# A three-layer interaction network on one core: reordering the preparation of its weights

## The chip, the core and the metric

The kernel runs on one core of a Trainium2 chip. The core has TensorE (PE, matrix products, which write to the accumulation memory PSUM), VectorE (DVE), ScalarE (ACT) and GpSimd (POOL) for element-wise work, SyncE (SP) as a further issuer of transfers, and 16 DMA engines that move data between DRAM and the on-chip memory SBUF. PSUM has eight banks of 128 rows by 512 float32 columns. The engines run on their own and wait for each other by semaphores. The metric is the device time of one execution in microseconds (us), the median of several runs; less is better.

## The reference

For each of 1024 samples there is a matrix X0 of 39 fields by 64 embedding columns. Three layers each form all products of a field of the layer's input with a field of X0 and mix them with weights. The sums over the embedding columns of all three layers go through one linear layer.

```python
B, F, E = (1024, 39, 64); HID = [64, 64, 64]        # B is 1024 in the inputs
def _cin_layer(Xk, X0, W, b):
    Wr = W.reshape(O, Hk, Fdim)
    return jnp.einsum('bhe,bfe,ohf->boe', Xk, X0, Wr) + b[None, :, None]
Xk = X0
for W, b in ((W0, b0), (W1, b1), (W2, b2)):
    Xk = _cin_layer(Xk, X0, W, b)
    outs.append(Xk.sum(axis=-1))
y = concatenate(outs, axis=-1) @ fc_w.T + fc_b
```

All data are float32. Only the sum over the last layer is wanted, so a kernel may multiply weights together beforehand: fc_w's last third into W2 gives a matrix v2 (64 by 39), v2 into W1 gives a table T (fields by fields by 64), and only W0 and T then meet the data.

## The kernel before

It has a prologue, which builds a table of weights `wa`, and a stream of main products, which multiplies `wa` by products of fields. The samples are taken in 32 blocks of 32 samples (2048 columns). For a block, GpSimd gathers rows of x into four rolled copies `r` (and, for two blocks at a time, `u` and `v`), VectorE multiplies two of them into a tile `p`, and TensorE multiplies `p` by one chunk of `wa` in four quarters of 512 columns, into four PSUM banks `po`. Six chunks belong to each block and a seventh, of half height, to two blocks.

The prologue, by engine in program order (cuts are marked):

```python
psum = tile_pool(name="psum", bufs=8, space=PSUM)      # eight banks, taken in turn
...
nc.vector.memset(ones, 1.0)
nc.vector.memset(zeros, 0.0)                            # 128 x 512
...
load(0)                                                 # x of block 0, on SyncE
nc.scalar.dma_start(fcrow, fc_w)
nc.scalar.dma_start(w2s, w2...)
load_ones(0, nc.scalar)
nc.scalar.dma_start(w0s[0:F], w0v[:, 0 : NW * H])       # NW = 20 fields
nc.sync.dma_start(w0s[H : H + F, ...], w0v[:, NW * H : F * H])
for s, engine in enumerate((nc.sync, nc.scalar)):
    engine.dma_start(w1s[H * s : H * s + H], w1[...])
...
def spin(n, to):                                        # a dummy product of zeros
    nc.tensor.matmul(to[:, 0:n], zeros[:, 0:128], zeros[:, 0:n], start=True, stop=True)
spin(512, pr)
...                                                     # index lists; GpSimd starts the gathers
nc.tensor.matmul(small[:, 0:1], fcrow2, one)            # fc turned into a column
nc.vector.tensor_scalar(fc2[:, 0::32], mask, small[:, 0:1], None, ALU.mult)
spin(128, pr)
for k in ...: turn_row(small[...], k)                   # five more turned rows
for k in range(2):                                      # v2 from W2: 2 banks x 4 column groups
    for u in range(4):
        nc.tensor.matmul(pv[k][32 * u : 32 * u + 32, 0:320], fc2[...], w2v[...])
for k in range(NW // 2):                                # W0 turned, alternating row groups
    for s in range(2):
        nc.tensor.transpose(pw[s][...], w0s[H * s : H * s + F, ...], unit[...])
...                                                     # v2 copied; more index lists
def untwine(half, a, n, src, width):
    for s, copy in enumerate((nc.vector.tensor_copy, nc.scalar.copy)):
        copy(bothv[H * half :..., a + s : a + n : 2, 0:width], src[H * s : H * s + H, ...])
for s, (a, n) in enumerate(((0, NW), (NW, F - NW))):
    untwine(0, a, n, pw[s], F)                          # W0 into `both`
for s in range(2):                                      # T = v2 x W1, fields 0 to 31
    for k in range(2):
        nc.tensor.matmul(pt[s][H * k : H * k + H], v2[rows], w1v[rows, NA * k : ...])
for s in range(2):                                      # fields 32 to 38, one bank for both s
    nc.tensor.matmul(pr[rows, 0 : 32 * NR], v2[rows], w1v[rows, 2 * NA : F, :])
spin(128, small)
for s, copy in enumerate(copies): copy(part[:, :, ...], pt[s]...)
for s, copy in enumerate(copies): copy(rest[:, :, ...], pr[H * s : ...]...)
for k in range(3):                                      # T turned: part, part, rest
    for a in range(0, n, 2): nc.tensor.transpose(to[...], src[rows, a : a + m, :], unit[...])
    untwine(1, NA * k, n, to, FT)                       # T into `both`
for _ in range(2): spin(256, small)
```

Then come the first three chunks. `weight_rows` adds entries of `both` into `pairs`, `weight_turn` turns that by TensorE and ScalarE copies it into `wa`:

```python
for k, (n, c) in enumerate(steps[:3]):
    weight_rows(c)
    if not k:
        weight_turn(c)
        spin(256, small)
    product(n, c, halves[0], p[n, c])                   # 1024 columns of p
for n, c in steps[:3]:
    product(n, c, halves[1], p[n, c])
n, c = steps[3]; weight_rows(c); p[n, c] = product(n, c)
for k, (n, c) in enumerate(steps[:3]):                  # TensorE: quarter 0, turn, quarter 1
    multiply(n, c, p[n, c], (0,))
    if k < 2: weight_turn(steps[k + 1][1])
    multiply(n, c, p[n, c], (1,))
...                                                     # quarters 2, 3; then all other chunks
```

Of the kernel before, what the change touches and what calls it, by code (L numbers as in the profile page):

```python
# [98 lines left out]
def cin_kernel(ctx: ExitStack, tc: tile.TileContext, x, w0t, b0, w1, b1, w2, b2, fc_w, fc_b, out):  # L99
# [72 lines left out]
    with prep as prep:  # L172
# [8 lines left out]
        ones = prep.tile([16, 2, 128], F32, name="ones")  # L181
        zeros = prep.tile([128, MM], F32, name="zeros")
        warm = prep.tile([1, 1], F32, name="warm")
# [7 lines left out]


        nc.vector.memset(ones, 1.0)
        nc.vector.memset(zeros, 0.0)  # L194
        nc.vector.memset(fc2, 0.0)
# [3 lines left out]
        def load_ones(k, engine):  # L199
            engine.dma_start(xd[k][F::FT].rearrange("r (p c) -> p r c", c=128), ones)  # L200

        load(0)
        nc.scalar.dma_start(fcrow, fc_w)
        nc.scalar.dma_start(w2s, w2.rearrange("o (s n) -> (o s) n", s=2))
        load_ones(0, nc.scalar)
        w0v = w0t.rearrange("b a h -> b (a h)")
        nc.scalar.dma_start(w0s[0:F], w0v[:, 0 : NW * H])
        nc.sync.dma_start(w0s[H : H + F, 0 : (F - NW) * H], w0v[:, NW * H : F * H])  # L208
        for s, engine in enumerate((nc.sync, nc.scalar)):
# [13 lines left out]

        pv = [bank("pv") for _ in range(2)]
        small = bank("small")
        pw = [bank("pw") for _ in range(2)]
        pt = [bank("pt") for _ in range(2)]
        pr = bank("pr")


        def spin(n, to):
            nc.tensor.matmul(to[:, 0:n], zeros[:, 0:128], zeros[:, 0:n], start=True, stop=True)  # L232

        spin(512, pr)


# [60 lines left out]
        nc.vector.tensor_scalar(unit, apart, 0, None, ALU.is_equal)  # L297
        spin(128, pr)
        for k in range(3):
            turn_row(small[0:H, k + 1 : k + 2], k)  # L300
        for k in range(2):
            turn_row(small[H:128, k + 4 : k + 5], k)

# [10 lines left out]
        for k in range(2):  # L314
            for u in range(4):
                f0 = u // 2 * 19 + k * 10
                nc.tensor.matmul(  # L317
                    pv[k][32 * u : 32 * u + 32, 0:320],
                    fc2[:, u % 2 * 32 : u % 2 * 32 + 32],
                    w2v[:, f0 : f0 + 10, :],  # L320
                    start=True,
                    stop=True,
                )

        for k in range(NW // 2):
            for s in range(2):
                n = min(128, (F - NW * s) * H - k * 128)
# [11 lines left out]
        for s in range(2):  # L339
            rows = slice(H * s, H * s + H)  # L340
            nc.vector.tensor_copy(v2[rows, 0:20], column[0:H])
            nc.scalar.copy(v2[rows, 20:F], column[H:128, 1:20])
        nc.scalar.copy(fc, small[0:H, 1:4])
        nc.scalar.copy(fc0s[H:128], small[H:128, 4:5])

# [18 lines left out]

        def untwine(half, a, n, src, width):

            for s, copy in enumerate(copies):
                m = (n + 1 - s) // 2
                copy(  # L369
                    bothv[H * half : H * half + H, a + s : a + n : 2, 0:width],  # L370
                    src[H * s : H * s + H, 0 : m * FT].rearrange("p (a b) -> p a b", b=FT)[
                        :, :, 0:width
                    ],
                )

        for s, (a, n) in enumerate(((0, NW), (NW, F - NW))):
            untwine(0, a, n, pw[s], F)
        w1v = w1s.rearrange("o (h f) -> o f h", f=F)
        for s in range(2):
            rows = slice(H * s, H * s + H)  # L380
            for k in range(2):
                nc.tensor.matmul(  # L382
                    pt[s][H * k : H * k + H],
                    v2[rows],
                    w1v[rows, NA * k : NA * (k + 1), :],
                    start=True,
                    stop=True,
                )
        for s in range(2):
            rows = slice(H * s, H * s + H)  # L390
            nc.tensor.matmul(  # L391
                pr[rows, 0 : 32 * NR], v2[rows], w1v[rows, 2 * NA : F, :], start=True, stop=True
            )
        spin(128, small)
        for s, copy in enumerate(copies):
            at = slice(32 * s, 32 * s + 32)
            copy(part[:, :, at], pt[s].rearrange("b (a h) -> b a h", h=32))
        for s, copy in enumerate(copies):
            at = slice(32 * s, 32 * s + 32)
            copy(  # L400
                rest[:, :, at],
                pr[H * s : H * s + H, 0 : 32 * NR].rearrange("b (a h) -> b a h", h=32),
            )
        for k in range(3):
            src = part if k < 2 else rest
            rows = slice(H * (k % 2), H * (k % 2) + FT)
            n = NA if k < 2 else NR
            to = (pv[0], pv[1], pr)[k]
            for a in range(0, n, 2):
# [5 lines left out]
                )  # L415
            untwine(1, NA * k, n, to, FT)
        for _ in range(2):
            spin(256, small)
        first = [prods.tile([128, BLK], F32, name="p", tag="p") for _ in range(3)]
# [131 lines left out]
    for k, (n, c) in enumerate(steps[:3]):  # L551
        p[n, c] = first[k]
        weight_rows(c)
        if not k:
            weight_turn(c)
            spin(256, small)
        product(n, c, halves[0], p[n, c])
    for n, c in steps[:3]:
# [100 lines left out]
```

## Time and profile before

| | |
|---|---|
| median of 3 runs | 751.73 us (751.16 to 751.74) |
| span of the profiled execution | 748.3 us |
| PE busy | 739.5 us (99%) |
| DVE busy | 643.5 us (86%) |
| ACT busy | 163.8 us (22%) |
| POOL busy | 319.3 us (43%) |
| mean DMA rate | 241 GB/s |
| mean granted TensorE clock | 0.995 |

Busy time is the time in which an engine has an instruction in work. Matmuls overlap and their ends are modelled, so a busy TensorE is not one at its peak. The page cuts the span in 40 slices, each of 18.7 us here, and gives the busy share of each in tenths. A row of the timeline gives start, length, engine, line of the kernel, operation, output and inputs, count, and in brackets the idle time before it with what ended it. Lines 369, 397, 400 and 411 are the copies into `both`, `part` and `rest` and the transposes of T; 382 and 391 are the products of v2 and W1; 328 the transposes of W0; 431 the sums in `pairs`; 466 and 467 the turned chunk and its copy; 482 the main products; 232 the dummies; 166 the products of fields.

### The profile page before, as it was taken

How to read it: one execution, taken by the hardware profiler on the slowest of the kernel's cores; microseconds unless marked ns; L12 is line 12 of the kernel's file. 1: busy time of each engine (PE TensorE's matmuls, PEld its weight loads, DVE VectorE, ACT ScalarE, POOL GpSimd, SP SyncE). 2: the span in 40 equal slices, each digit the busy share in tenths (PEclk: the TensorE clock that was granted, in tenths of full speed). 3: DMA queues.
4: the chain of work that ended last, by engine and by line, in shares of the span. 5: the costliest groups of instructions: out<-in, count | busy, mean ns of one | idle time of the engine just before them, and what ended most of it. 6: DMA issues, size and time to landing. Idle time of an engine off the chain costs nothing.

```text
span 748.3 us, 5266 instructions
## 1 busy us (share of the span) xinstructions
PE 739.5 (99%) x1903; PEld 322.7 (43%) x1903; DVE 643.5 (86%) x509; ACT 163.8 (22%) x223; POOL 319.3 (43%) x193
## 2 busy tenths in 40 slices
PE   7999999999999999999999999999999999999998
PEld 3444444444444444444444444444444444444443
DVE  5998899888889888898888889888899888898885
ACT  2132211221212222212221212222112221212222
POOL 5778633336353253633436243263532436243100
PEclk8999999999999999999999999999999999999999
DMA  8789975875757776575875757776565855737400
GB/s 268 270 304 412 330 290 171 330 259 205 289 164 280 252 293 250 178 294 176 338 255 201 288 166 281 259 278 252 185 275 202 336 224 179 295 138 288 168 1 0
DMA packets 58791, 180.07 MB, mean 241 GB/s; under 512 B 37079, under 2 KB 37176, under 8 KB 38669
## 3 DMA queue, kind: packets, MB, share of 16 engines
q0 software_dynamic: 24160, 169.39, 59.6%
q1 hardware_dynamic: 34277, 9.17, 5.3%
q10 hardware_dynamic: 328, 1.18, 0.6%
q8 instruction: 15, 0.25, 0.1%
q14 instruction: 11, 0.09, 0.0%
HBM read 179.66 MB, written 10.28 MB: 254 GB/s over the span
## 4 chain that ended last, share of the span: by engine, by line
PE 97%; DMA 1%; DVE 0%; issue 0%; SPq 0%; ACT 0%
PE po L482 96%; DMA w1s<-in_w 1%; PE pv L411 0%; PE pt L382 0%; PE small L232 0%; PE tr L466 0%; SPq L118 0%; ACT both L369 0%; PE pr L391 0%; SPq L208 0%; DVE g L521 0%; DVE sums L523 0%; ACT zq L520 0%; DVE pairs L431 0%; DVE both L369 0%
## 5 line engine op out<-in xcount | busy, mean ns | idle before, releaser
L482 PE MATMUL po<-p,wa 128*128 128x512 f32 (+1 forms) x1792 | 721.9, 595 | 0.0
L166 DVE TENSOR_TENSOR p<-r 128x2048 f32<-128x2048 f32 (+1 forms) x195 | 434.8, 2257 | 85.4 <-PE po L482 84.6
L482 PEld LDWEIGHTS po<-p,wa 128*128 128x128 f32 (+1 forms) x1792 | 313.5, 190 | 405.0 <-issue 383.5
L125 POOL DMA_INDIRECT r<-xd,lists x131 | 256.3, 1956 | 361.1 <-DVE p L166 330.7
L501 ACT ACTIVATE z<-po,fc0s 64x512 f32<-64x512 f32 x124 | 84.7, 683 | 356.4 <-PE po L482 349.5
L495 ACT COPY g<-u 39x1024 f32<-39x1024 f32 x64 | 66.6, 1043 | 180.7 <-DVE sums L512 180.6
L507 DVE SCALAR_TENSOR_TENSOR g<-po,b0s,z 64x512 f32<-64x512 f32 x124 | 86.4, 734 | 0.0
L512 DVE TENSOR_REDUCE sums<-g 103x16 f32<-103x1024 f32 x62 | 75.6, 1220 | 2.2
L125 POOL DMA_INDIRECT u<-xd,lists x16 | 33.0, 2062 | 9.8 <-DMA xd<-in_x 5.2
L168 DVE TENSOR_TENSOR p<-u,v 128x2048 f32<-128x2048 f32 x16 | 36.6, 2285 | 0.0
L125 POOL DMA_INDIRECT v<-xd,lists x16 | 20.3, 1269 | 4.9 <-issue 4.9
L521 DVE SCALAR_TENSOR_TENSOR g<-po,b0s,zq 64x512 f32<-64x512 f32 x4 | 3.0, 743 | 5.3 <-ACT zq L520 5.3
L467 ACT COPY wa<-tr 128x128 f32<-128x128 f32 x7 | 1.9, 266 | 18.9 <-PE tr L466 18.9
L431 DVE TENSOR_TENSOR pairs<-both 128x6 f32<-128x6 f32 (+27 forms) x50 | 5.4, 177 | 0.4 <-ACT both L369 0.4
L118 POOL DMA_DIRECT2D xd<-in_x x5 | 5.2, 1047 | 0.0
L520 ACT ACTIVATE zq<-po,fc0s 64x512 f32<-64x512 f32 x4 | 2.7, 683 | 10.2 <-PE po L482 10.2
L232 PE MATMUL pr<-zeros 128*128 128x512 f32 (+1 forms) x4 | 2.9, 822 | 1.7 <-DVE zeros L194 1.7
L232 PE MATMUL small<-zeros 128*128 128x256 f32 (+1 forms) x8 | 3.7, 591 | 0.0
L382 PE MATMUL pt<-w1s,v 64*64 64x512 f32 x8 | 2.2, 1107 | 1.4 <-DMA w1s<-in_w 1.4
L334 DVE STREAM_TRANSPOSE blocks<-pv 128x320 f32<-128x320 f32 x2 | 1.0, 516 | 2.2 <-PE pv L317 2.2
L523 DVE TENSOR_REDUCE sums<-g 103x8 f32<-103x512 f32 x4 | 2.7, 686 | 0.1
L610 PE MATMUL py<-sums,wfin 103*1 103x512 f32 (+2 forms) x6 | 2.1, 448 | 0.6 <-DVE sums L523 0.6
(95 smaller groups left out, 43.8 us busy)
## 6 DMA issues: line engine op xcount, KB each, us to landing
xd<-in_x SPq DMA_DIRECT2D x27, 312.0 KB
r<-xd,lists POOLq DMA_INDIRECT x131
xd<-in_x POOLq DMA_DIRECT2D x5, 312.0 KB
w2s<-in_w ACTq DMA_DIRECT2D x1, 624.0 KB
w1s<-in_w ACTq DMA_DIRECT2D x1, 312.0 KB
w1s<-in_w SPq DMA_DIRECT2D x1, 312.0 KB
u<-xd,lists POOLq DMA_INDIRECT x16
v<-xd,lists POOLq DMA_INDIRECT x16
```

Of the source, the lines that this page charges most:

```text
L118: engine.dma_start(xd[n // 2 % NTAB][first : first + F].rearrange("f (b e) -> f b e", e=E), xv[:, n * BB : (n + 1) * BB, :],)
L125: nc.gpsimd.indirect_dma_start(dst[:, cols], None, table, bass.IndirectOffsetOnAxis(ap=lists[:, k : k + 1], axis=0), element_offset=cols.s ...
L166: nc.vector.tensor_tensor(p[:, cols], r[:, i, cols], r[:, k, cols], ALU.mult)
L168: nc.vector.tensor_tensor(p, ut[n // 2 % 2], vt[n // 2 % 2], ALU.mult)
L232: nc.tensor.matmul(to[:, 0:n], zeros[:, 0:128], zeros[:, 0:n], start=True, stop=True)
L431: nc.vector.tensor_tensor(out, diagonal(a, b, sa, sb), diagonal(b, a, sb, sa), ALU.add)
L482: nc.tensor.matmul(po[n + h][m], wa[w, c, :], p[w, bass.ts(m, MM)], start=c == opens[n + h], stop=c == closes[n + h],)
L495: nc.scalar.copy(gt[H : H + F], ut[n // 2 % 2][h : h + F, bass.ts(m, SUB)])
L501: nc.scalar.activation(z[m // 2][:, bass.ts(m % 2, MM)], po[n][m][H:128], AF.Identity, bias=fc0s[H:128])
L507: nc.vector.scalar_tensor_tensor(gt[0:H, at], po[n][m][0:H], b0s, z[m // 2][:, at], ALU.add, ALU.mult)
L512: nc.vector.tensor_reduce(sums[:, b_at : b_at + SB], gt.rearrange("p (b e) -> p b e", e=E), AX.X, ALU.add)
L521: nc.vector.scalar_tensor_tensor(gt[0:H], po[n][m][0:H], b0s, t, ALU.add, ALU.mult)
```

## The change

It reorders the prologue and leaves the main stream and the arithmetic as they are. Its aims are these.

- W2 goes first on ScalarE's queue and the small fc row to SyncE's, so that W2 and, behind it, W1 arrive sooner. Both parts of W0 go on ScalarE's queue.
- W0's transposes run one row group after the other and no longer alternate.
- The last seven fields of T are multiplied, copied and turned first. Each row group of these products gets its own bank.
- Each copying engine gets a bank of its own: VectorE unpacks one and ScalarE the other, where before both shared each bank. The fields of the first 32 come in another order so that each engine's copies cover a connected range of fields.
- All dummies have 256 columns, write to a bank `idle` that nothing else uses, and come in pairs. `zeros` is half as wide and is set first.
- The turned rows of fc come after W2's products, and the copies of them to SBUF after the first three half products.
- The first product of fields is cut in two of 512 columns, so that TensorE's first quarter has its data sooner.

The diff, cut to its core:

```diff
-        zeros = prep.tile([128, MM], F32, name="zeros")
+        zeros = prep.tile([128, MM // 2], F32, name="zeros")
+        nc.vector.memset(zeros, 0.0)
         nc.vector.memset(ones, 1.0)
-        nc.vector.memset(zeros, 0.0)
...
+        nc.sync.dma_start(fcrow, fc_w)
+        nc.scalar.dma_start(w2s, w2.rearrange("o (s n) -> (o s) n", s=2))
         load(0)
-        nc.scalar.dma_start(fcrow, fc_w)
-        nc.scalar.dma_start(w2s, w2.rearrange("o (s n) -> (o s) n", s=2))
         load_ones(0, nc.scalar)
-        nc.scalar.dma_start(w0s[0:F], w0v[:, 0 : NW * H])
-        nc.sync.dma_start(w0s[H : H + F, 0 : (F - NW) * H], w0v[:, NW * H : F * H])
+        for s, n in enumerate((NW, F - NW)):
+            nc.scalar.dma_start(w0s[H * s : H * s + F, 0 : n * H], ...)
...
+        pt = [bank("pt") for _ in range(2)]
+        idle = bank("idle")
+        pw = [bank("pw") for _ in range(2)]
         small = bank("small")
-        pw = [bank("pw") for _ in range(2)]
-        pt = [bank("pt") for _ in range(2)]
-        pr = bank("pr")
...
+        def spin(n=1):
+            for _ in range(n):
+                nc.tensor.matmul(idle[:, 0 : MM // 2], zeros[:, 0:128], zeros, start=True, stop=True)
+        spin(2)
...
-        spin(128, pr)
-        for k in range(3): turn_row(...)            # these five go behind W2's products
+        spin(2)
...
-        for k in range(NW // 2):
-            for s in range(2):
+        for s in range(2):
+            for k in range(NW // 2):
                 nc.tensor.transpose(pw[s]...)
...
         for s, (a, n) in enumerate(((0, NW), (NW, F - NW))):
-            untwine(0, a, n, pw[s], F)
+            untwine(copies[s], 0, a, n, 1, pw[s], F)
+        for s in range(2):
+            nc.tensor.matmul(pv[s][rows, 0 : 32 * NR], v2[rows], w1v[rows, 2 * NA : F, :])
         for s in range(2):
             for k in range(2):
                 nc.tensor.matmul(pt[s][H * k : H * k + H], v2[rows],
-                    w1v[rows, NA * k : NA * (k + 1), :])
+                    w1v[rows, NA * k : NA * (k + 1), :].rearrange("o (t j) h -> o j t h", t=2))
-        for s in range(2):
-            nc.tensor.matmul(pr[rows, 0 : 32 * NR], v2[rows], w1v[rows, 2 * NA : F, :])
-        spin(128, small)
-        # copies: part from pt, then rest from pr; turned and unpacked: part, part, rest
+        # copies: rest from pv, then part from pt
+        turn_fields(pt[0], rest, slice(0, FT), NR)
+        untwine(copies[0], 1, 2 * NA, NR, 1, pt[0], FT)
+        for k in range(2):
+            turn_fields(pw[k], part, slice(H * k, H * k + FT), NA)
+        for k in range(2):
+            untwine(copies[k], 1, NA * k, NA, NA // 2, pw[k], FT)
+        spin(2)
...
             weight_turn(c)
-            spin(256, small)
-        product(n, c, halves[0], p[n, c])
+            spin()
+            for m in range(2):
+                product(n, c, slice(m * MM, (m + 1) * MM), p[n, c])
+        else:
+            product(n, c, halves[0], p[n, c])
+    nc.scalar.copy(fc, small[0:H, 1:4])
+    nc.scalar.copy(fc0s[H:128], small[H:128, 4:5])
```

## The prediction

> **What bounds the kernel now.** I read the page first, for who is busy, then the chain of waits, then the timeline of the first 40 us.
>
> ```profile
> PE   7999999999999999999999999999999999999998
> PEclk8999999999999999999999999999999999999999
> L482 PE MATMUL po<-p,wa 128*128 128x512 f32 (+1 forms) x1792 | 721.9, 595 | 0.0
> ```
>
> The main products (line 482) fill 721.9 of 748.3 us with no idle time in front. They are 896 products in two records each. A full one advances the timeline by 0.86 us (two records of 0.43), so nothing that the change does not touch can shrink: its arithmetic stays. What is left is the first slice of PE, the 7, and the clock, the 8. The chain of waits, cut to that stretch (start, length, what):
>
> ```profile
> 2.62 7.63 DMA w1s<-in_w
> 10.25 0.75 issue
> 11.00 2.18 PE pt L382 x8
> 13.18 0.82 PE pr L391 x4
> ...
> 15.31 2.27 PE pv L411 x16
> ...
> 19.27 0.58 DVE pairs L431 x5
> ...
> 21.29 1.19 PE po L482 x2
> ```
>
> So the prologue is one chain: W1 lands, is multiplied by v2, turned, unpacked into `both`, added into `pairs`, and the first main product leaves at 21.12 us. The ends of matmuls are modelled, so I take true ends from who could start on them. From the timeline:
>
> ```profile
> 8.83 0.79 PE L328 MATMUL pw<-unit,w0s 39*128 39x39 f32 x20 [0.55 <-DMA w0s<-in_w0t]
> 11.77 1.03 DVE L369 COPY both<-pw 64x390 f32<-64x390 f32 x2 [1.09 <-remote]
> 13.92 0.69 DVE L397 COPY part<-pt 128x512 f32<-128x512 f32 x1 [1.13 <-PE pt L382]
> 14.67 0.58 ACT L397 COPY part<-pt 128x512 f32<-128x512 f32 x1 [1.39 <-PE pr L391]
> 16.79 0.38 DVE L400 COPY rest<-pr 64x224 f32<-64x224 f32 x1 [2.18 <-PE pv L411]
> 17.21 0.34 ACT L400 COPY rest<-pr 64x224 f32<-64x224 f32 x1 [1.96 <-issue]
> 17.60 0.88 DVE L369 COPY both<-pv 64x320 f32<-64x320 f32 x2 [0.43 <-PE pv L411]
> 19.13 0.71 DVE L431 TENSOR_TENSOR pairs<-both 128x36 f32<-128x36 f32 x6 [0.41 <-ACT both L369]
> 19.76 1.22 DVE L166 TENSOR_TENSOR p<-r 128x1024 f32<-128x1024 f32 x1
> ```
>
> Three things are to be seen. VectorE, idle for 1.09 us, reads W0's transposes only at 11.77, so 20 of them, alternating between two row groups, took 11.77 - 8.83 = 2.9 us, 0.145 us each, and W1's products, ready at 11.00, really ran from about 11.7. VectorE then waits for `rest` until 16.79, over 2 us after `pt` was readable (14.67): the small product into the shared bank `pr` was late. And ScalarE's copies start just behind VectorE's (17.21 after 17.17).
>
> **What the Trainium skill says.** "TensorE: Matmul & The Clock Gate", Part 1: the clock is halved by default, judged in free-running windows of about 3.4 us, and sustained activity releases it. The trace agrees: the granted clock is 0.50 from 11.4 to 14.8 and from 18.2 to 21.65 us, full between and after. "TensorEngine Tiling (Array Packing)", Gotcha 1: different row tiles cannot access one PSUM bank at the same time. The late `pr`, written by both row groups, is in keeping with it; the trace doesn't prove it. "PSUM — Partial Sum Buffer", PSUM bank collisions: engines must be kept apart by bank and quadrant; the tight order of the two copies of `pr` agrees. "DMA: Bandwidth & Descriptors", Queues, rings and completion order: each DMA engine serves its queues in turn, packet by packet. In the trace x's first 256-byte packets move at 4.28 us, just before W2's last end (4.74), although x was issued first.
>
> **The change, part by part.**
>
> W2 and W1 sooner. W2's issue moves to the head of ScalarE's queue, 1.27 to 0.74 us, fcrow goes to SyncE. From 2 to 10 us the DMA engines are 0.84 to 1.08 busy in the table by stage, and the bytes are the same, so the whole train moves by about 0.5: W1 is usable at 10.5 instead of 11.0, and x with its gathers also about 0.5 sooner.
>
> W0 group by group. The four transposes of `rest` (17.61, 0.41 us, one row group) suggest 0.23 us latency and 0.06 each after that. At that pace 20 cost 1.4 us, and with W0's second half landing near 9.0 they end near 10.2, ahead of W1. W1's products then start at 10.5 instead of 11.7: 1.2 us sooner.
>
> Last fields first, bank per row group. `rest` is 224 columns in two passes. At the slow clock a 512-column pass takes 0.85 us (the first dummy: two passes and about 0.37 latency are its 2.08), so these take 2 x 0.37 = 0.75. `pt` needs 14.67 - 11.7 = 2.95 until ScalarE may read, as before. So ScalarE's copy of `part` starts at 10.5 + 0.75 + 2.95 = 14.2 (before 14.67) and ends at 14.8 (0.58). What is won at the start is mostly spent on `rest` in front, but the 2 us of `pr` behind it vanish: `rest` is copied near 11.7, beside `pt`.
>
> Transposes and unpacking. Sixteen transposes: 14.8 + 0.23 + 16 x 0.063 = 16.05. Then each engine has its own bank and its own range of fields; ScalarE's two copies (0.42 each) end at 16.9. `pairs` starts near 16.95 instead of 19.13: 2.2 us sooner.
>
> Half of the first product. `pairs` 0.71, then 512 columns instead of 1024 (half of 1.22, 0.61): the first main product goes at 16.95 + 0.71 + 0.61 + 0.1 = 18.4 instead of 21.12, 2.7 us sooner. Not all of that is kept. VectorE must deliver three sets of `pairs` and three half products before the third chunk's product; before, this took from 19.13 to 24.80, 5.7 us, so now it is ready at 16.95 + 5.7 = 22.65. TensorE took it at 25.1 before. That is 2.4 us sooner, and from there I count TensorE as unbroken again.
>
> Dummies. Columns of dummies go from 1280 to 1792. In front of W2 they cost nothing as long as W2 lands no sooner (about 4.6); the two pairs later sit in waiting time. The copies of fc and fc0s (0.15 each) and the turned rows (0.82 for five) leave the path to W2, onto time in which TensorE waits for W1.
>
> Sum if all of it works: 2.4 us. Discounts: 40% that transposes cost 0.14 each whatever their order (two groups of 16 and 10 on the path: about 1.2 us back, 0.5 expected), and a clock that may be slow behind 18.2, below, with little of it expected net, since before also began in slow clock. I predict 1.9 us off: 751.73 - 1.9 = 749.8.
>
> **The rivals.**
>
> Transposes are bound by their weight loads. They read 0.139 us each in the load rows, and 16 of them from 15.31 to 17.60 is 0.14 too. Against it stand the four of `rest`. If it holds, W0 ends near 11.3, `part`'s last transpose near 17.2, `pairs` starts at 18.1, and the time is about 750.8.
>
> The clock falls. With dummies ending early (after the last transposes, not beside the copies), the window from 14.8 to 18.2 may be half empty, as before's was (it lost the clock at 18.2). Then the first four quarters run at 1.7 instead of 0.86 us up to 21.65, TensorE and no longer VectorE is late at the third chunk by about 1.2 us, and the time is about 750.6. For the change: its dummies are longer. If instead the clock is full from 14.8 on, and W1's products too run full, the time is near 748.5.
>
> The gathers of block 1 become the bound. In the timeline its second product starts at 42.82 after 0.63 us on the DMA of r. This landing moves only 0.5 while the rest moves 2. But counting 0.86 per product TensorE takes that chunk near 49.9, and it is ready at 45.1; 4.8 of reserve, so 2 to 3 are left. If I am wrong there, gathers eat the whole gain: 751.5.
>
> W1 is not sooner, as packets of x or of the gathers go first: the gain shrinks by 0.5, to 750.3.
>
> **Range and chances.** All rivals that I see give 748.5 to 751.5; three runs of before span 0.6. I give 748.2 to 751.3 for 8 in 10. A change of 2% is 15 us, and the whole prologue in front of the first main product is 21 us, so faster by that much is out of reach (0.005); slower needs a stream that breaks later on (0.01). Within 2%: 0.985.
>
> **What would show it.** Right: W1's products near 10.5; VectorE's copy of `pw` ready before 10.5; `rest` copied before `part`; `pairs` near 17; first main product near 18.4, with one gap of a few tenths before the third chunk; main products unchanged at 722 us or a little above. Each step is wrong if its time stays where it was: transposes of `part` still 2.2 us long, W1's products still at 11, or a clock of 0.50 behind 18.2. The prediction fails as a whole if TensorE waits for r or for products beyond 25 us, or if the prologue's saving passes 3.5 us.

## The result and the profile after

The kernel after takes 751.41 us (median of four runs, 749.11 to 752.54), beside 751.74 of the kernel before on the same chip: ratio 0.9993 with a 95% interval of 0.9969 to 1.0018. A later measurement with 13 runs of after and 51 of before gives 750.65 against 751.23, 0.9990 (0.9982 to 0.9998). So the change takes off 0.1%, about 0.6 us, where 1.9 were predicted. Only the second interval excludes no change, and barely.

From the page of the kernel after, the same two rows that the prediction began with:

```profile
PE   7999999999999999999999999999999999999998
PEclk8899999999999999999999999999999999999999
```

TensorE is as full as before. The second slice of the clock, 18.75 to 37.5 us, has fallen from 9 to 8. The rest of the answer lies again in front of the first main product. The chain of waits up to there (start, length, what):

```profile
2.15 9.83 DMA w1s<-in_w
...
12.12 0.74 PE pv L383 x2
...
15.17 0.76 issue
15.93 0.38 PE pt L409 x4
16.31 0.78 PE pw L409 x16
17.09 1.65 PE idle L233 x4
...
18.76 0.43 ACT both L371
...
19.80 0.59 DVE pairs L434 x5
...
21.82 1.71 PE po L485 x2
```

W1 is longer on its way (9.83 us, before 7.63) and its products start at 12.12 instead of 11.00. The 16 transposes of `part` are short, 0.78 us. Then comes a piece that has no business here: 1.65 us "PE idle L233", dummy products, and ScalarE leaves only behind them. The timeline (start, length, engine, line, operation, and in brackets the idle time before it and who ended it):

```profile
8.67 1.30 PE L329 MATMUL pw<-unit,w0s 39*128 39x39 f32 x20
10.01 0.94 ACT L371 COPY both<-pw 64x390 f32<-64x390 f32 x2 [0.42 <-PE pw L329]
11.77 1.17 POOL L125 DMA_INDIRECT r<-xd,lists  x1 [8.67 <-DVE both L371]
13.18 0.38 DVE L398 COPY rest<-pv 64x224 f32<-64x224 f32 x1 [1.53 <-PE pv L383]
15.09 0.69 DVE L404 COPY part<-pt 128x512 f32<-128x512 f32 x1 [1.52 <-PE pt L389]
15.20 0.59 ACT L404 COPY part<-pt 128x512 f32<-128x512 f32 x1 [1.55 <-PE pt L389]
16.98 0.99 DVE L371 COPY both<-pw 64x320 f32<-64x320 f32 x2
18.76 0.86 ACT L371 COPY both<-pw 64x320 f32<-64x320 f32 x2 [2.97 <-PE idle L233]
19.66 0.72 DVE L434 TENSOR_TENSOR pairs<-both 128x36 f32<-128x36 f32 x6 [1.68 <-ACT both L371]
21.62 1.91 PE L485 MATMUL po<-p,wa 128*128 128x512 f32 x2
```

Half of the plan works. W0's transposes are read at 10.01 (before 11.77), `rest` at 13.18 (16.79) and `part`'s products by ScalarE at 15.20 (14.67), although W1 came 1.1 us later. The second bank of `part`'s transposes undoes it: VectorE reads the first at 16.98, ScalarE's copy of the second, turned 0.3 us behind it, starts at 18.76. `pairs` starts at 19.66 (19.13) and the first main product at 21.62 (21.12). The first row gather is issued at 11.77; the prediction had it half a microsecond sooner than in before, where its row is:

```profile
7.44 1.17 POOL L125 DMA_INDIRECT r<-xd,lists  x1 [4.34 <-DMA xd<-in_x]
```

From the table by stage (stretch, its length, busy time and count of PE, PEld, DVE, ACT and POOL, granted TensorE clock, DMA share, GB/s), two stretches of after and then one of before:

```profile
18.00:21.40 3.40, 1.03 (x4) 0.69 (x4) 1.74 (x8) 1.44 (x6) 2.87 (x3) 0.50 0.87 287
21.40:24.85 3.45, 3.45 (x6) 1.66 (x6) 3.45 (x19) 0.66 (x4) 1.18 (x1) 0.50 1.07 377
21.60:25.00 3.40, 3.40 (x10) 1.34 (x9) 3.40 (x14) 0.53 (x2) 2.30 (x2) 0.99 0.53 183
```

The clock is 0.50 from 18.0 to 24.85 us in after; in before it is 0.50 from 18.2 to 21.64 and full behind it. So the main products of after ran at half clock for their first 3.2 us, those of before for 0.5.

**One sum that holds for every trace.** The third chunk's first product is the point from which the prediction took TensorE as unbroken. I read its start from each trace and take it from that execution's own time:

| profiled execution | first main product | third chunk | its time | time minus third chunk |
|---|---|---|---|---|
| before | 21.12 | 25.11 | 750.06 | 724.95 |
| after | 21.62 | 26.88 | 751.83 | 724.95 |
| again (after, once more) | 21.71 | 26.82 | 751.77 | 724.95 |
| dma_before | 23.48 | 27.91 | 752.86 | 724.95 |
| no_late_dummy | 21.51 | 27.41 | 752.38 | 724.97 |
| before_w0_grouped | 21.65 | 26.53 | 751.49 | 724.96 |
| after_gathers_held | 26.26 | 32.34 | 757.28 | 724.94 |
| dense_end | 20.97 | 25.32 | 750.34 | 725.02 |
| before_four_gathers | 19.53 | 23.34 | 749.53 | 726.19 |
| four_gathers_hold_by_act | 19.19 | 23.01 | 748.04 | 725.03 |

The four traces left out of the table give 724.95, 724.97, 724.96 and 726.34. From the third chunk on everything is 725.0 us, to a tenth, but for two traces with 1.2 and 1.4 more, which are explained below. A prologue's microsecond is worth a full microsecond, and "hidden later on" is no answer here. The table also shows that the page of before belongs to one of its shorter executions, 750.06 against a median of 751.73, and that of after to one 0.4 above its median: two traces must be compared with their own times, not with the medians.

### The profile page after: what moved, and what is told of

It is laid out like the page before. It is cut to its first block, busy times and chain, and to the rows that moved or that the text cites. A ratio compares the mean times of both kernels' runs of the same rounds, so it can differ in the third digit from the quotient of the medians.

```text
span 750.1 us, 5270 instructions
## 1 busy us (share of the span) xinstructions
PE 740.6 (99%) x1905; PEld 324.1 (43%) x1905; DVE 643.9 (86%) x511; ACT 163.8 (22%) x222; POOL 324.4 (43%) x193
## 4 chain that ended last, share of the span: by engine, by line
PE 97%; DMA 1%; DVE 0%; issue 0%; ACT 0%; SPq 0%; ACTq 0%
PE po L485 96%; DMA w1s<-in_w 1%; PE idle L233 0%; PE pt L389 0%; PE tr L469 0%; SPq L118 0%; PE pv L383 0%; ACT both L371 0%; PE pw L409 0%; DVE g L524 0%; DVE sums L526 0%; ACT zq L523 0%; DVE pairs L434 0%; PE pt L409 0%; SPq L203 0%
## 5 line engine op out<-in xcount | busy, mean ns | idle before, releaser
L166 DVE TENSOR_TENSOR p<-r 128x2048 f32<-128x2048 f32 (+2 forms) x196 | 434.9, 2247 | 86.3 <-PE po L485 83.6
L125 POOL DMA_INDIRECT r<-xd,lists x131 | 265.2, 2025 | 357.1 <-DVE p L166 325.2
L125 POOL DMA_INDIRECT u<-xd,lists x16 | 32.3, 2022 | 10.5 <-DMA xd<-in_x 5.9
L125 POOL DMA_INDIRECT v<-xd,lists x16 | 17.2, 1074 | 4.9 <-issue 4.9
L233 PE MATMUL idle<-zeros 128*128 128x256 f32 x14 | 6.3, 591 | 1.2 <-DVE zeros L193 1.2
L523 ACT ACTIVATE zq<-po,fc0s 64x512 f32<-64x512 f32 x4 | 2.7, 684 | 10.2 <-PE po L485 10.2
L469 PE MATMUL tr<-unit,pairs 128*128 128x128 f32 x7 | 2.2, 319 | 2.4 <-DVE pairs L434 2.4
L233 PEld LDWEIGHTS idle<-zeros 128*128 128x128 f32 x14 | 3.6, 289 | 1.7 <-DVE zeros L193 1.2
```

Source lines behind the costliest of these rows:

```text
L125: nc.gpsimd.indirect_dma_start(dst[:, cols], None, table, bass.IndirectOffsetOnAxis(ap=lists[:, k : k + 1], axis=0), element_offset=cols.s ...
L166: nc.vector.tensor_tensor(p[:, cols], r[:, i, cols], r[:, k, cols], ALU.mult)
L233: nc.tensor.matmul(idle[:, 0 : MM // 2], zeros[:, 0:128], zeros, start=True, stop=True)
L469: nc.tensor.transpose(tr[:, at], pairs[:, c], unit)
```

## The experiments

The first theory was that the order of the transfers is to blame. The packets suggest it. x is read in 1248 packets of 256 bytes on SyncE's queue. In before they move from 4.29 to 6.08 us; W0's second half stands behind them in the same queue. In after both halves of W0 (packets of 4864 and 5120 bytes) are on ScalarE's queue and run beside x, whose packets now take from 3.90 to 10.06 us; W1's lower half, behind x, ends at 11.10 instead of 9.9. The prediction had cited the Trainium skill for this ("DMA: Bandwidth & Descriptors", Queues, rings and completion order: each DMA engine turns between its queues packet by packet) and hadn't drawn the consequence for a queue of small packets. One for one it is not in this trace: until 7.0 us 1060 of x's packets move beside 97 of about 5 KB. Nor is it the same each time: the last 188 of x's packets trickle in until 10.06, and in two later traces with the same transfers (no_late_dummy and dense_end) the last ends at 8.80 and 8.34 and the gathers start at 10.10. The rivals were the dummies (which the chain names) and, for the late banks of before, the alternation that the prediction blamed. The first four kernels ran side by side on one chip.

### again

No edit: the kernel after, for the spread and a second trace.

> The changed kernel once more, unchanged, to see what separates its quick executions from its slow ones. Clock theory: the executions fall into groups by the mean granted clock; about 0.993 (two halved windows in a row behind 18 us) goes with 751.5 to 752.5 us and 0.995 with 749 to 751, a difference of 1.5 us or more. Transfer theory: the groups do not follow the clock; the time follows when W1 lands, 12.0 us in the profile at hand.

Measured: 750.65 us, ratio 0.9990 (0.9982 to 0.9998). The second trace repeats the first: ScalarE's last copy at 18.86, `pairs` at 19.75, first main product at 21.71. The clock theory holds in kind: seven executions at a mean clock of 0.993 average 751.53 us, five at 0.995 average 750.29, so 1.2 us apart and not 1.5.

### dma_before

After, with the transfers in the order of before.

```
-  sync: fcrow, x, w1 low        scalar: w2, ones, w0 (both halves), w1 high
+  sync: x, w0 second half, w1 low   scalar: fcrow, w2, ones, w0 first half, w1 high
```

> The changed kernel with the transfers issued as before the change (x first on SyncE, fcrow, W2, ones and W0's first part on ScalarE, W0's second part on SyncE). Transfer theory: x lands near 6.6 us instead of 10.9, the first gather starts near 7.5 instead of 11.8, W1 is usable near 10.9 instead of 12.0, and the time falls by about 1 us, to about 750.3. Clock theory alone: W1 lands sooner but the time stays within 0.5 us, scattered by the clock as before. My prediction's own reading, by which the new order brings W1 sooner: slower by 0.5 us.

Measured: 752.39 us, ratio to before 1.0011 (1.0003 to 1.0020), so 1.7 us slower than after. The gathers start at 7.74 as expected; W1's products start at 11.60, sooner than in after (12.12) but later than the 10.9 expected; and the time went the other way. Its timeline:

```profile
7.74 1.17 POOL L125 DMA_INDIRECT r<-xd,lists  x1 [4.64 <-DVE blocks L335]
12.78 1.14 DVE L371 COPY both<-pw 64x390 f32<-64x390 f32 x2 [2.13 <-PE pv L383]
16.39 0.94 ACT L371 COPY both<-pw 64x390 f32<-64x390 f32 x2 [5.79 <-remote]
16.43 0.38 DVE L398 COPY rest<-pv 64x224 f32<-64x224 f32 x1 [2.51 <-remote]
17.87 0.69 DVE L404 COPY part<-pt 128x512 f32<-128x512 f32 x1 [1.05 <-remote]
21.52 0.72 DVE L434 TENSOR_TENSOR pairs<-both 128x36 f32<-128x36 f32 x6 [0.35 <-ACT both L371]
23.48 1.80 PE L485 MATMUL po<-p,wa 128*128 128x512 f32 x2
```

W0's transposes, 1.16 us of work from 9.30, are read at 12.78 and 16.39; `rest`, whose products start at 11.60, at 16.43. "<-remote" means that the profile names no engine as the releaser. So the theory "late x and late W1 cost the time" falls as the main cause: with the gathers 4 us and W1 0.5 us sooner it got worse. The suspicion is now that something that goes with the early gathers delays TensorE's results.

### no_late_dummy

After, without the two dummies behind the last transposes (which the chain of waits named).

```
             untwine(copies[k], 1, NA * k, NA, NA // 2, pw[k], FT)
-        spin(2)
```

> The changed kernel without the pair of dummies behind the transposes of part. Dummy theory: the second group of transposes is readable for ScalarE only at 18.74 us, 1.9 after the first, because the dummies behind it are in the way; without them it is readable near 17.3, pairs starts near 18.3 instead of 19.66, and the time falls by up to 1 us or what the clock leaves of it. Rival, the delay lies elsewhere: ScalarE still starts near 18.7 and the time stays or rises, as the clock now has less to see and the window behind 18 us is at 0.50 in every execution (mean clock 0.993).

Measured: 751.11 us, ratio 0.9998 (0.9991 to 1.0006). In the timeline:

```profile
18.66 0.86 ACT L371 COPY both<-pw 64x320 f32<-64x320 f32 x2 [2.98 <-remote]
```

The second bank is read at 18.66 with no dummy behind it, so the chain's entry named the wrong one. The record puts the end of the second bank's transposes at 16.97; ScalarE's wait ended 1.7 us behind it. The chain, built on modelled ends, had filled this gap with what TensorE did next.

### before_w0_grouped

Before, with W0's transposes by row group and nothing else.

```
-        for k in range(NW // 2):
-            for s in range(2):
+        for s in range(2):
+            for k in range(NW // 2):
                 nc.tensor.transpose(pw[s]...)
```

> The kernel before with W0's transposes one row group after the other, nothing else. Alternation theory: both groups are readable near 10.2 us instead of 11.77, W1's products then run from W1's landing, part is readable for VectorE near 13.2 instead of 13.92 and for ScalarE near 13.9 instead of 14.67, and 0.7 us are saved, 751.0 us. Rival, the late reading has another cause than alternation: VectorE still reads near 11.7 and the time stays at 751.7.

Measured: 751.50 us, ratio 1.0001 (0.9993 to 1.0010). The second group of W0 in the timeline:

```profile
12.31 0.56 DVE L369 COPY both<-pw 64x390 f32<-64x390 f32 x1 [1.17 <-PE pw L328]
```

The first group is read at 10.59, but the second, for which 1.16 us of work began at 9.77, at 12.31, and `rest` at 16.61 as in before. Grouping alone doesn't make the results prompt.

What was common to all late banks: they fall into the stretch in which GpSimd issues the six half-width gathers of block 0 (before 7.44 to 14.83, dma_before 7.74 to 15.12, after 11.77 to 19.17), or shortly behind it. VectorE's and ScalarE's signals were prompt in the same stretch. The reverse doesn't hold: of the seven signals of after that tell VectorE or ScalarE of a product between 12 and 19 us, five came within 0.02 us of the end in the records. The late ones are the second bank of `part`'s transposes, by 1.65, and one product of `part`, by 0.69. The next three kernels, on a second chip, take the gathers away from the stretch. (When TensorE signals is read from the semaphore events of the traces.)

### after_gathers_held

After, with all gathers, and the other transfers that follow them on GpSimd's queue, behind the last copies into `both`; two copies of one element hold the queue.

```
-        for cols in halves: roll(0, (0, 1, 2), cols)      # and the later gathers
...
         for k in range(2):
             untwine(copies[k], 1, NA * k, NA, NA // 2, pw[k], FT)
+        for a in range(2):
+            nc.gpsimd.tensor_copy(hold[..a..], bothv[H : H + 1, NA * a : NA * a + 1, 0:1])
+        for cols in halves: roll(0, (0, 1, 2), cols)      # and the later gathers
```

> The kernel after, with every row gather on GpSimd moved behind the two last copies of T into the table both (a one-element GpSimd copy of each of them holds the queue). Theory that the gathers make TensorE's results readable late: the second group of part's transposes, which ended at 16.86 by the record and was readable at 18.74, is now readable within 0.1 us of its end, so ScalarE's copy starts at about 17.0 instead of 18.76; the gathers then start near 18, and the first main product, which now waits for gathered rows, starts at 22 to 24. Theory that the lateness belongs to the burst of 16 transposes itself: still readable at 18.6 to 18.8.

Measured: 757.28 us (one run), since the rows now come late; what counts is the timeline in front:

```profile
15.66 0.94 PE L397 MATMUL pw<-unit,part 40*128 40x40 f32 x16
16.64 0.86 ACT L359 COPY both<-pw 64x320 f32<-64x320 f32 x2 [1.33 <-PE pw L397]
17.63 0.72 DVE L437 TENSOR_TENSOR pairs<-both 128x36 f32<-128x36 f32 x6
```

ScalarE reads the second bank at 16.64, at the end of the transposes (16.60). `pairs` starts at 17.63 instead of 19.66; 0.4 of this belongs to W1, which came that much sooner in this run (products at 11.68).

### before_gathers_held

The same hold in the kernel before, alternation and shared bank unchanged.

> The kernel before (W0's transposes alternating between the row groups, the five last fields last and in one shared bank), with every row gather moved behind the last copies into both. Theory that the gathers make the results late: W0's transposes, which were readable 2.1 us after their end in the kernel before, are readable at about 10.0 instead of 12.2; the bank of the five last fields, 2.8 us late before, is on time; all T copies are done near 16.5 to 17.5 instead of 18.8. Theory of the prediction (alternation of row groups, and one bank shared by two of them): the lateness stays at 2 us and 2.8 us.

Measured: 756.95 us (one run), and in the timeline:

```profile
9.18 0.79 PE L324 MATMUL pw<-unit,w0s 39*128 39x39 f32 x20 [0.88 <-DVE v L337]
10.53 1.02 DVE L357 COPY both<-pw 64x390 f32<-64x390 f32 x2
13.98 0.38 DVE L388 COPY rest<-pr 64x224 f32<-64x224 f32 x1 [0.25 <-PE pr L379]
15.02 0.88 DVE L357 COPY both<-pv 64x320 f32<-64x320 f32 x2 [0.65 <-PE pv L399]
16.54 0.71 DVE L434 TENSOR_TENSOR pairs<-both 128x36 f32<-128x36 f32 x6 [0.41 <-ACT both L357]
25.79 2.04 PE L485 MATMUL po<-p,wa 128*128 128x512 f32 x2 [7.65 <-DVE p L166]
```

TensorE's signals for both banks of W0 come at 9.98 and 10.01 (VectorE, busy until then, reads at 10.53), the one for `pr` at 13.96, at once. The old arrangement has `pairs` at 16.54, sooner than the prediction hoped for from the new one (16.95). So neither alternating row groups nor one bank shared by two of them cost anything that this trace shows. The gathers did, or what goes with them; the next run divides the two. The two held traces also compare the arrangements without the gathers: from the start of W1's products to `pairs` the old one takes 5.60 us (10.94 to 16.54), the new one 5.95 (11.68 to 17.63). So on this way the reordering itself wins nothing.

### before_gathers_narrow

As before_gathers_held, but at the old place stand seven gathers of 16 columns each, 1/64 of the bytes or less (the full ones follow later).

```
+        for cols in halves:
+            roll(0, (0, 1, 2), slice(cols.start, cols.start + 16))
+        roll(0, (3,), slice(0, 16))
```

> As the run before_gathers_held, but at the old place stand the seven first gathers with 16 columns each instead of 1024 or 2048, so GpSimd works on the same seven lists at the same time and moves 1/64 of the bytes (the full gathers follow, held back). If the transfers of the gathered rows make TensorE's results late, W0's transposes are readable at about 10.0 and all is on time, as with the gathers held. If GpSimd's own work on the lists does it, the lateness of 2.1 us at W0's transposes and 2.8 us at the five last fields comes back.

Measured: 759.30 us (one run). The timeline:

```profile
7.92 1.18 POOL L125 DMA_INDIRECT r<-xd,lists  x1 [4.68 <-DVE blocks L333]
9.51 0.79 PE L327 MATMUL pw<-unit,w0s 39*128 39x39 f32 x20 [1.24 <-DMA w0s<-in_w0t]
12.16 1.03 DVE L360 COPY both<-pw 64x390 f32<-64x390 f32 x2 [1.52 <-remote]
15.11 0.38 DVE L391 COPY rest<-pr 64x224 f32<-64x224 f32 x1 [1.05 <-PE pr L382]
17.98 0.88 DVE L360 COPY both<-pv 64x320 f32<-64x320 f32 x2 [2.49 <-PE small L232]
19.51 0.71 DVE L437 TENSOR_TENSOR pairs<-both 128x36 f32<-128x36 f32 x6 [0.41 <-ACT both L360]
```

The lateness is back with almost no bytes: W0 at 12.16 again, `part`'s transposes (ended 16.23 by the record) at 17.98, `pairs` 3.0 us later than with the gathers held. A narrow gather keeps GpSimd as long as a half-width one, 0.95 us and 0.30 between two. (`rest` is the exception, 0.8 us late where 2.8 were expected.) It isn't the number of packets either: the seven narrow gathers move 112 packets of 512 bytes, where those of before have begun 751 of 4096 bytes by 19.0 us. Nor is it the other transfers of GpSimd's queue, which are still held. So it is GpSimd's work on the lists, not the rows' bytes. How it reaches TensorE, and whether the products themselves or only their signals are late, isn't shown by any view. The Trainium skill's "SBUF — State Buffer", Who interferes with whom, has TensorE waiting on nobody. It speaks of the ports of SBUF; whether a port makes the results late here isn't shown, but in this trace they are late.

### dense_end

After, with dummies in the two stretches in which TensorE idles behind 14.6 us.

```
             copy(part[:, :, at], pt[s]...)
+        spin(2)
...
             untwine(copies[k], 1, NA * k, NA, NA // 2, pw[k], FT)
-        spin(2)
+        spin(5)
```

> The kernel after with two more dummy products between the products of part and the transposes of T (15.2 to 15.9, where TensorE was idle), and five instead of two behind the transposes, to reach from 17.0 to about 20. Theory that half-clock windows of 3.4 us behind thin stretches eat the gain: the window that begins near 18.0 or at the latest the one near 21.4 is granted full clock, the first main products take 0.43 us a record instead of 0.85, and the time falls by 1.2 to 1.7 us to about 749.5 (ratio to before 0.9975). If the clock does not follow the dummies, or something else paces the first products, the time stays at 750.7 to 751.4.

Measured, on the chip of the three held runs: 750.34 us, 0.9999 (0.9990 to 1.0008). The timeline:

```profile
18.55 0.86 ACT L371 COPY both<-pw 64x320 f32<-64x320 f32 x2 [3.44 <-remote]
19.45 0.71 DVE L435 TENSOR_TENSOR pairs<-both 128x36 f32<-128x36 f32 x6 [0.68 <-ACT both L371]
20.97 1.12 PE L486 MATMUL po<-p,wa 128*128 128x512 f32 x2
```

The clock follows: full from 14.86 on in the profiled execution, and the granted mean of the runs rises to 0.997 from 0.9935 for before. The time is not shown to follow; after itself wasn't timed on this chip. `part`'s second bank is late again (18.55, with the gathers at their old place on the chip where it was prompt with them held), `pairs` starts at 19.45, and VectorE needs 5.72 us from there to the end of the third half product (25.17), the 5.7 that the prediction had taken from before; TensorE starts the third chunk at 25.32. With a full clock VectorE is the pace of this stretch. In after, where it was half, VectorE had the third chunk's half product ready at 25.39 and TensorE started it at 26.88: 1.5 us, of which 0.15 remain at full clock, so the clock cost about 1.3 us of that execution.

### before_four_gathers

If the lists count, fewer lists should help. The kernel before, block 0's six half-width gathers made three of full width, the gathers for later tables held as above. A third chip, on which neither before nor after was traced.

```
-        for cols in halves:
-            roll(0, (0, 1, 2), cols)
+        roll(0, (0, 1, 2))
         load(1, nc.gpsimd)
         roll(0, (3,))
```

> The kernel before with block 0's six half-width gathers made into three of full width (four gathers in all instead of seven, of the same bytes), and the gathers of the later tables held behind the last copies of T. The list work of the narrow run made signals late with 1/64 of the bytes, so what should count is how many lists GpSimd works off and until when: the first three now end near 11.1 instead of 14.8, the fourth near 13.5. Theory of list work: W0's transposes stay late (readable 11.7 to 12.2), but the bank of the five last fields is readable at 14 to 15 instead of 16.8 and part's transposes at 16 instead of 17.6; the pairs start at 17.0 to 18.0 instead of 19.1, the first main product at 19 to 20 instead of 21.1, the time falls by 1 to 2 us to 749 to 750. If the bytes count after all, the lateness stays as in the kernel before and the first products wait for rows: first main product at 21 or later, time 751 to 753.

Measured: 750.48 us against 751.49, ratio 0.9989 (0.9979 to 1.0000). The timeline:

```profile
12.05 1.03 DVE L360 COPY both<-pw 64x390 f32<-64x390 f32 x2 [1.40 <-remote]
14.28 0.38 DVE L391 COPY rest<-pr 64x224 f32<-64x224 f32 x1 [0.25 <-PE pr L382]
16.00 0.88 DVE L360 COPY both<-pv 64x320 f32<-64x320 f32 x2 [1.35 <-PE pv L402]
17.53 0.71 DVE L433 TENSOR_TENSOR pairs<-both 128x36 f32<-128x36 f32 x6 [0.41 <-ACT both L360]
19.53 1.10 PE L484 MATMUL po<-p,wa 128*128 128x512 f32 x2 [0.40 <-DVE p L166]
22.13 4.94 POOL L410 COPY hold<-both 1x1 f32<-1x1 f32 x2 [8.38 <-DVE pairs L433]
45.92 2.41 PE L484 MATMUL po<-p,wa 128*128 128x512 f32 x5 [1.09 <-DVE p L166]
```

As expected W0 is late while the first three lists are worked off (to 11.39; signalled at 12.03), and from then on all is prompt, beside the fourth list (12.76 to 13.75) too: `rest` at 14.28, the transposes at 16.00, first main product at 19.53. The time was expected at 749 to 750. Of the 1.8 us by which its third chunk is sooner than in the trace of before, 1.2 are lost at 45.92, the larger sum in the table: the cause is my hold. `both` is complete at 17.5, but GpSimd's two one-element copies start at 22.13, because GpSimd's queue first waits for the landing of block 0's last gather, at 21.98 by its semaphore (the row names VectorE's sums, which end at nearly the same time). They then stand beside VectorE's products until 27.07; the next three gathers are issued from 27.34 at about 3 us each, and TensorE waits for the rows. The skill's "SBUF — State Buffer", Who interferes with whom, says that a VectorE operation with two inputs in SBUF blocks a GpSimd operation that reads SBUF. The hold read SBUF, and this agrees with it: the pair of copies took 4.94 us, and 0.55 in before_gathers_held.

### after_four_gathers_x_first

dma_before with the same four gathers and hold.

> The kernel after with the old order of the transfers (x ahead, as in the run dma_before, so the gathers start at 7.7) and with four gathers for block 0 instead of seven, the later tables held behind T's last copies. Theory of list work: the gathers end near 13.7 instead of 16.5; W0's transposes stay late, by 2.5 us or more, but the five last fields are readable before 15 (16.4 in the run dma_before) and part's transposes within 0.3 us of their end, near 16.5; first main product 19.5 to 20.5 instead of 23.5, time 749.5 to 750.5 (752.39 in dma_before). If it is the bytes or the transfers that matter, it stays at 752 or above.

Measured beside the last: 750.60 us, 0.9993 (0.9984 to 1.0001), with the same loss behind 45 us. `rest` is read by 13.20 (16.43 in dma_before), both banks of `part`'s transposes by 16.60, first main product at 19.43 (23.48). W0's transposes are 1.2 to 1.4 us late where 2.5 or more were expected; in all else up to the first main product the theory of the lists passes in both arrangements. With the lists short the new arrangement (19.43) and the old one (19.53) are level.

### four_gathers_hold_by_act

before_four_gathers with another hold: ScalarE writes one element into the gathers' target.

```
-        for a in range(2): nc.gpsimd.tensor_copy(hold[..a..], bothv[..])
+        nc.scalar.copy(ut[0][0:1, 0:1], bothv[H : H + 1, 2 * NA + 1, 0:1])
```

> As before_four_gathers, but the gathers of the later tables are held by a one-element ScalarE write into their target instead of by a GpSimd copy. In before_four_gathers GpSimd's copy stood until 22.13 beside VectorE's work and the next gathers were issued from 27.3 on with 3 us each, and the 64th main product came 1.2 us later, against the 48th, than in the kernel before. If the hold caused that wait: gathers of u and v at 17.6 to 20, no extra wait between the 48th and the 64th main product, first main product again at 19.5, time 749.2 to 749.8. If the wait comes from elsewhere: the 64th main product stays at 45.9, time 750.5.

Measured, on a fourth chip: 748.12 us, and there the kernel before takes 748.00: ratio 0.9998 (0.9990 to 1.0006). The wait at 45 us is gone (the sum is 725.03 again), first main product at 19.19. But there is nothing to win on this chip. W0's transposes are signalled at 9.94 with the gathers running from 7.68, on time, as all else in this trace. The likely reading is that the lateness doesn't exist on this chip, so that before hasn't lost those 2 us either. In keeping with it, executions of before with a mean clock of 0.995 average 748.90 us here (12) and 750.76 on the chip of the first four runs (23). But before wasn't traced here, so this is argued and not shown.

### w1_before_w0

The last one with W1's transfers ahead of W0's, W0's transposes behind W1's products, and without the dummy of 128 columns that stood there.

> As four_gathers_hold_by_act, with W1's transfers put ahead of W0's and W0's transposes behind the products of part and rest. Theory that W1's landing sets the way to the first main product: W1 is usable near 9.5 instead of 11.2, the products of part start there, T's last copies end 1 to 1.7 us sooner, first main product 18 to 18.7, time 748.0 to 748.8. Rival, from the list work: the products now end at 11.5, while the gathers are issued (7.7 to 13.7), so they become readable late by 1.5 us or more, and first main product and time stay within 0.4 us of four_gathers_hold_by_act.

Measured beside the last: 749.02 us, 1.0009 (1.0003 to 1.0016). W1's products start at 9.43 and are prompt, `pairs` is at 16.72 (17.20), 0.5 us sooner and not 1 to 1.7, and the first main product at 18.70. But TensorE's clock is 0.50 from 17.5 to 20.9, the third chunk comes at 23.52 (23.01), and the rest is 725.0 as always. This execution loses to a window of the clock what its prologue won; whether the missing dummy has a part in it isn't shown.

## Why the prediction was right in kind and wrong in size

Right: the class (the same within 2%), the stage that decides, TensorE unbroken behind the third chunk, VectorE's 5.7 us up to it (19.66 to 25.39), and the rival "the clock falls", which came with 1.3 us (1.2 foreseen), though for two windows instead of one. The time of 751.41 lies 0.1 above the stated range, and that it lies so near is luck, as the step of the base shows. By its own steps:

- **W1 usable at 10.5.** Failed: 12.1 in the profiled execution. "The bytes are the same, so the whole train moves" left out that x's small packets share the engines with W0's large ones once these are in another queue. This is shown only in part: with the old order back (dma_before) the products start at 11.60, not at 11.00, and with the new order they start between 11.45 and 12.12 in five traces. 1.6 us of the miss at this step; 0.6 came back, as `rest` and `part` took 3.1 us to ScalarE instead of the 3.7 counted. The count rested on the reading that W1's products of before "really ran from about 11.7" for 2.95 us; that was a late signal, and with the gathers held they start at 10.94 and are signalled 2.2 us later. Net 1.0 (ScalarE's copy of `part` at 15.20, predicted 14.2).
- **W0 by group ends near 10.2.** The number held (read at 10.01), the cause didn't. The alternating form is as prompt with the gathers held (signalled at 10.01), and the grouped one is late with the gathers early (12.31). The rival of 0.14 us a transpose fails: the 20 of after took 1.3 us by the record, 0.065 each, and were signalled at once.
- **The shared bank makes `pr` late.** Failed as a cause: with the gathers held the same bank is prompt (13.96). `rest` came sooner in after, although W1 came later, because x, and with it the gathers, came 4.3 us later: with the gathers early again (dma_before) it is read at 16.43.
- **Transposes and unpacking from 14.8 to 16.9.** Failed in size: 15.8 to 19.6, 3.8 us instead of 2.1. The transposes took 0.78, but the second bank was readable 1.65 us late, because the gathers now stood beside it. This is the largest term. Together with W1: 1.0 + 1.7 = 2.7, all of 19.66 - 16.95.
- **1.45 us from `pairs` to the first product.** 1.96, as dummies and the turn ran at half clock (1.52 at full clock in dense_end). That makes 3.2 in all (21.62 - 18.4).
- **Third chunk at 22.65.** 26.88: 3.2 from above and 1.0 more, again from the clock.
- **The base.** The steps were counted from a trace of a 750.06 us execution and taken from a median of 751.73. By the sum above, third chunk plus 725.0, a median execution of before has its third chunk near 26.8, not 25.11. Taken from the trace's own 750.06, the same working gives 748.2. Errors of 4.2 us in the steps, 1.7 in the base and the discount of 0.5 partly cancelled: 4.2 - 1.7 - 0.5 = 2.0, the 751.83 of the traced execution less 749.8.
- **The dummies.** The columns before are 1536 (512, two times 128, three times 256), not 1280; no later step used the figure.

The step that failed, then, is the cause given for the late results of before, bank and order, and with it most of the 2.2 us by which `pairs` was to come sooner. The lateness goes with GpSimd's lists. An estimate from single traces of different chips: beside the held ones it costs 2.5 us at `pairs` in before (19.13 against 16.54, less 0.1 for W1) and 1.6 in after (19.66 against 17.63, less 0.4 for W1). So 0.9 was won there; W1 came 1.1 later, and the new arrangement itself takes 0.35 more: `pairs` starts 0.5 later. Which of this leaves 0.6 us in the medians isn't shown, as no execution of before near its median was traced.

## What to carry to other kernels

Read when a consumer could start, not when TensorE's record ends, and put all late signals on one time axis with the other engines' work before giving them a local cause: here bank, order and dummies were each plausible and each wrong, and holding one engine back in both kernels, then giving it the lists without the bytes, settled which work it was. When a change of queues delays a transfer "nobody waits for", ask what its successor will then stand beside. Take a trace together with its own time: with an unbroken main stream, one start time plus a constant gives each run to a tenth of a microsecond.

## What the runs showed of the hardware that was not expected

- While GpSimd worked through lists of gathers, TensorE's signals came up to 5.9 us behind the end in the records on three chips; with 1/64 of the bytes by up to 2.0; with the gathers held back within 0.1 us, but for one product of `part` that was 0.7 behind there too. On a fourth chip none was late. The lists alone don't suffice: in after the products of `rest` were prompt beside them, and so were long main products later on. Besides the lists, each late stretch has a run of ten or more short products (W0's or `part`'s transposes, or the turned rows of fc) at or shortly ahead of its first long delay; whether that is a condition wasn't tested. The way of this inside the chip stays open.
- A queue of 1248 packets of 256 bytes needed 1.8 us beside one other queue's tail, and 6.2, 5.0 and 4.4 us beside packets of about 5 KB (after, no_late_dummy, dense_end).
- The mean granted clock differs between executions of one kernel and sorts its times: on one chip before took 750.76 us on average at 0.995 (23 runs), 751.36 at 0.993 (19), 752.04 at 0.992 (6), 752.34 at 0.990 (3).
- The same kernel, before, has medians of 751.23, 750.78, 751.49 and 748.00 us on four chips.
